# Block turns on VectorE in place of TensorE turns for sixteen row tiles of a sparse attention layer

## The chip, the cores and the metric

The kernel runs on one core of one Trainium2 chip. A core has five engines that run side by side, each through its own list of instructions in order: TensorE (PE in the profile; its weight loads are PEld), VectorE (DVE), ScalarE (ACT), GpSimd (POOL) and SyncE (SP), which here only issues transfers. Transfers are queued by SP, ScalarE or GpSimd and run on 16 DMA engines. Data lies in SBUF, 128 partitions wide; TensorE writes to PSUM, from which VectorE and ScalarE read.

The metric is the device time of one execution in microseconds.

## The reference

The input x has 2708 rows of 1024 numbers, adj is a 2708 by 2708 matrix of zeros and ones in which about 0.15% are ones (some four in a row), and there are three 1024 by 1024 weights with biases.

```python
h = jnp.maximum(_layernorm(x, axis=-1), 0.0)
q = h @ W_q.T + b_q
k = h @ W_k.T + b_k
v = h @ W_v.T + b_v
z = (1.0 / math.sqrt(1024)) * (q @ k.T)
spare_z = z * adj_tensor
spare_z = jnp.where(spare_z == 0.0, -10000.0, spare_z)
attn = jax.nn.softmax(spare_z, axis=1)
x = x + jax.nn.relu(attn @ v)
```

All but a few entries of a row of attn vanish, so a row of the result is a weighted sum of the few rows of h that adj names, times W_v.

## The kernel before, in words

**Stages.** First W_q and W_k are multiplied into one matrix M (lines 433 to 588). Meanwhile rows of x are normalised into h (`stats`, `root`, `apply`, `keep`), and VectorE searches the rows of adj for their ones (`found`, L376; `listed`, L389 to L395). Then h times M gives q, the scores are products of q with gathered rows of h (`scores`, L826), the sums u are weighted sums of gathered rows (`sums`, L879), and u times W_v, plus x, is the output. Rows are worked on in tiles of 128; there are 22 tiles.

**Units.** The products h times M and u times W_v run in units of two tiles, `units`, L1160: ten units q for the pairs (0,1) to (18,19), then ten units o for the pairs (6,5), (4,3), (2,0), (1,7), (13,12), (11,10), (14,9), (15,16), (20,17), (18,19), and tile 8 alone at the end. A unit is a 2 by 2 block product after Strassen and Winograd with seven products in place of eight. Each product is a block of eight matmuls (`add_block`, L948). Its left factors are a11, a12 (of the pair's first tile xa), a22 and a21 (of the second, xb), turned so that the 1024 columns lie on partitions, and the sums s1 = a22 + a21, s3 = a11 - a21, s2 = s1 - a11 and s4 = a12 - s2.

**Turning.** `half_turned` (L397) turns half a tile with four matmuls against the unit matrix (L402) into PSUM. `blocks` (L677) makes the factors for a pair: `upper` has a11 and a12 copied to SBUF by ScalarE (L684), `lower` has a22 copied and forms s1 and s3 on VectorE straight from PSUM (L688), and s2 and s4 on VectorE, or on GpSimd for the pairs (2,3) and (4,5) (L701, L702).

**Order.** `multiply` (L982) writes the order of a unit: the blocks on s2, a12, s4, s3, then the next unit's a11 and s1 (`opened`, L953), then a22. Between them it calls `after(i)`, i from 0 to 6 (L1172), which emits all that runs beside: `upper` for the next pair at i = 0 and `lower` at i = 2 (for the next pair of unit 0 at 3 and 4, of unit 3 at 4 and 5, L1200 to L1206), steps of the search (`steps_at`, L735), and `advance(share)` (L937), which hands out the attention stream on VectorE in portions of 20/7 us (q) or 19/7 us (o) a call. VectorE executes in the order in which this is written (`manual_schedule`), ScalarE and GpSimd too in the early part; TensorE, SP, and the others later, are ordered by a planner. When rows are loaded two units ahead (`load_rows`, L1130), the stream is driven on until their tiles are done (L1214).

**Rows.** The early tiles 0 to 7 keep their h tile in SBUF (`kept`, L217) until `natural_rows` (L716) hands them to units 0 to 3. Later q pairs are gathered from `h_dram`. Of the u tiles, those that are used within two units stay in SBUF (`near`, L933); ten others (6, 5, 4, 3, 2, 0, 1, 20, 18, 19) are stored to `u_dram` by SP (L888) and loaded again by SP (L1142). Row tiles share seven buffers (`row_tile`, L198).

**Search loads.** Rows of adj are loaded by SP into three buffers in turn (`loaded`, L342), so the load for one tile waits until the search three tiles earlier has let go of its buffer.

Of the kernel before, what the change touches and what calls it, by code (L numbers as in the profile page):

```python
# [10 lines left out]
FT = mybir.dt.float32  # L11
# [3 lines left out]
AF = mybir.ActivationFunctionType  # L15
# [18 lines left out]
FAR = 20.0  # L34
WIDE = 8
MOMENTS = (0, 1, 2, 3, 6, 7)
ROOT = 32
# [26 lines left out]
def tile_preln_masked_attention(  # L64
# [35 lines left out]

    h_dram = dram.tile([N, D], FT, name="h_dram")
    q_dram = dram.tile([EARLY * P, D], FT, name="q_dram")
    q_late = dram.tile([(BARE - EARLY) * P, D], FT, name="q_late")
# [97 lines left out]
    def stats(group):  # L201
# [6 lines left out]
        for i, t in enumerate(group):  # L208
            t0, n = tiles[t]
            if 15 <= t < 18:  # L210
                xt = work.tile([P, D], FT, tag="q", name=f"x_{t}", bufs=4)
            elif t >= FULL - 1:
                xt = work.tile([P, D], FT, tag="hT", name=f"x_{t}", bufs=2)
            else:
                xt = row_tile(f"x_{t}")
            if t < EARLY:
                kept[t] = xt  # L217
            nc.sync.dma_start(xt[:n], x[t0:t0 + n, :])
            xs.append(xt)
            if t in MOMENTS:  # L220
                continue
            st = stat.tile([P, NH, 6], FT, tag="st", name="st")
            for s in range(NH):
                nc.vector.bn_stats(st[:n, s, :], xt[:n, s * NB:(s + 1) * NB])
            nc.vector.bn_aggr(mv[:n, i, :], st[:n].rearrange("p s k -> p (s k)"))
# [31 lines left out]
    def apply(first, only=range(4)):  # L257

        group, xs, r = normed[first]
        for i in only:  # L260
            if i < len(group):
                n = tiles[group[i]][1]
                nc.scalar.activation(xs[i][:n], xs[i][:n], AF.Relu, bias=r[:n, 4, i:i + 1], scale=r[:n, 3, i:i + 1])

# [410 lines left out]
    behind = []  # L675

    def blocks(xa, xb, eng=None):  # L677

# [7 lines left out]
        def put(name, a, b, op, eng=None):  # L686
            ops[name] = small(name).rearrange("p (c q) -> p c q", q=P)
            step = (eng or nc.vector).tensor_tensor(ops[name], a, b, op=op)  # L688
            if eng is None:
                behind.append(step)  # L690

        def upper():
            held("a11", half_turned(xa, 0))
            held("a12", half_turned(xa, 1))

        def lower():
            held("a22", half_turned(xb, 1))
            a21 = half_turned(xb, 0)
            put("s1", ops["a22"], a21, ALU.add)
            put("s3", ops["a11"], a21, ALU.subtract)  # L700
            put("s2", ops["s1"], ops["a11"], ALU.subtract, eng)  # L701
# [6 lines left out]
    def banks_for(row):  # L708
# [5 lines left out]
        return return_  # L714

    def natural_rows(n):  # L716
        rows_of[n] = [kept.pop(t) for t in (2 * n, 2 * n + 1)]

    natural_rows(0)
    ops_of = {0: blocks(*rows_of.pop(0))}  # L720
# [154 lines left out]
    def sums(t):  # L875
# [8 lines left out]
        g_of.pop(t)  # L884
        if near(t):
            held[t] = u
# [243 lines left out]
    def load_rows(unit):  # L1130
        kind, *pair = unit
        rows = []
        for t in pair:
# [6 lines left out]
            else:  # L1140
                assert t in done, (t, done)
                nc.sync.dma_start(rows[-1], u_dram[t * P:(t + 1) * P, :])  # L1142
        return rows
# [16 lines left out]
    for n, unit in enumerate(units):  # L1160
        kind, ta, tb = unit
        now[0] = n
        if n == FIRST:
            ordered.close()
            ordered.enter_context(tc.manual_schedule(engines={mybir.EngineType.DVE}))
            nc.sync.dma_start(bp_dram, bp_sb[0:1, :])
        turn = n in (0, FIRST - 1)
# [313 lines left out]
```

## Time and profile before

| what | us |
|---|---|
| median of three runs | 644.58 |
| lowest, highest | 644.18, 644.96 |
| span of the profiled execution | 641.9 |
| TensorE busy | 635.2 |
| VectorE busy | 521.9 |
| GpSimd busy | 377.3 |
| ScalarE busy | 279.6 |

The page of the profiled execution gives its span, from the first to the last instruction, 641.9 us; its time with what lies around the span isn't listed apart from the three runs. The granted TensorE clock was 0.998 of full speed.

In the rows below, a line of the chain of waits has the start in us, the length in us, the engine, what is written, the line of the kernel and the count. A row of a timeline has start and length in us, then engine, line, operation, output and inputs, and in brackets how long the engine sat idle just before and what ended that. A group's row ends with busy us, mean ns of one, and the idle time before. A row of waits has the total us, the count and the longest. A row of stretches has from:to, its length, the busy us of PE, PEld, DVE, ACT and POOL with counts, the clock, the share of the DMA engines and GB/s. A row of transfers ends with KB each and the median us from issue to landing.

### The profile page before, as it was taken

To read this page: it belongs to the slowest core of one execution; us is meant where nothing else is said; L and a number is where in the kernel's file an instruction comes from. 1 tells how busy PE (TensorE), PEld (TensorE's weight loads), DVE (VectorE), ACT (ScalarE), POOL (GpSimd) and SP (SyncE) were. 2 spreads that over 40 slices of the span, in tenths; PEclk is the share of its full clock that TensorE was granted. 3 is DMA by queue.
4 is the path that set the end of the run, shared out by engine and by line. 5 is a ranking of instruction groups with operands and counts; after the bars stand their busy time and mean duration, and the time that the engine had idled before them with its cause. 6 is when DMAs were issued, how large, how long until landed. Compare 5 with 4: busy or idle time off the path is not lost.

```text
span 641.9 us, 6381 instructions
## 1 busy us (share of the span) xinstructions
PE 635.2 (99%) x1731; PEld 326.2 (51%) x1731; DVE 521.9 (81%) x1014; ACT 279.6 (44%) x426; POOL 377.3 (59%) x400
## 2 busy tenths in 40 slices
PE   9999999999999999999999999999999999999996
PEld 5777766444544444444444454454454444444442
DVE  5999788997895755998888959997999989989121
ACT  3539974849775622423223132433342344333300
POOL 2649960875858457755735525665685856872431
PEclk9999999999999999999999999999999999999999
DMA  8999997598798969998977998988898989995542
GB/s 338 407 366 314 345 346 295 189 358 301 264 358 317 363 201 404 355 359 257 322 260 275 419 416 267 327 272 255 240 328 272 283 331 304 281 285 125 146 139 95
DMA packets 61986, 189.02 MB, mean 294 GB/s; under 512 B 10701, under 2 KB 11037, under 8 KB 61048
## 3 DMA queue, kind: packets, MB, share of 16 engines
q0 software_dynamic: 27888, 84.95, 41.6%
q1 hardware_dynamic: 29994, 89.36, 37.7%
q10 hardware_dynamic: 4062, 14.24, 5.9%
q8 instruction: 16, 0.26, 0.2%
q14 instruction: 26, 0.21, 0.1%
HBM read 159.81 MB, written 42.31 MB: 315 GB/s over the span
## 4 chain that ended last, share of the span: by engine, by line
PE 98%; DMA 1%; DVE 0%; POOL 0%; POOLq 0%; issue 0%
PE ps L948 45%; PE psy L948 32%; PE ps_y L463 6%; PE pt L402 6%; PE ps_x L463 4%; PE ps_z L463 4%; DMA wlow<-in_wq_dram 1%; PE ps_h L1153 0%; PE ps_v L581 0%; DVE y_alone L1297 0%; POOL out_dram L1281 0%; POOLq L1303 0%; PE ps_all L664 0%; PE ps_in L662 0%; PE ps_b L728 0%
## 5 line engine op out<-in xcount | busy, mean ns | idle before, releaser
L597 POOL DMA_INDIRECT g<-h_dram,tab x105 | 124.8, 1188 | 70.4 <-ACT u L871 19.1
L948 PE MATMUL ps<-M,a 128*128 128x512 f32 x320 | 144.0, 593 | 0.0
L948 PE MATMUL psy<-wlow,s 128*128 128x512 f32 x320 | 143.9, 592 | 0.0
L826 DVE SCALAR_TENSOR_TENSOR junk<-g,pq 128x1024 uint8<-128x1024 f32 x93 | 114.0, 1226 | 9.8 <-DMA g<-h_dram,tab 7.3
L879 DVE SCALAR_TENSOR_TENSOR u<-g,coef,u 128x1024 f32<-128x1024 f32 x79 | 101.4, 1283 | 5.6 <-ACT u L871 3.7
L948 PEld LDWEIGHTS ps<-M,a 128*128 128x128 f32 x320 | 59.3, 190 | 68.0 <-issue 67.4
L948 PEld LDWEIGHTS psy<-wlow,s 128*128 128x128 f32 x320 | 59.2, 190 | 66.8 <-issue 65.8
L376 DVE FIND_INDEX8 at<-ones,adj 128x8 uint32<-128x685 f32 (+1 forms) x88 | 74.5, 865 | 0.0
L948 PE MATMUL psy<-wlow,a 128*128 128x512 f32 x160 | 71.9, 592 | 0.0
L948 PE MATMUL ps<-M,s 128*128 128x512 f32 x160 | 71.9, 592 | 0.0
L948 PE MATMUL ps<-wlow,s 128*128 128x512 f32 x160 | 71.9, 592 | 0.0
L355 ACT ACTIVATE sized<-adj 128x2708 uint8<-128x2708 f32 (+1 forms) x22 | 54.3, 2468 | 7.7 <-DMA adj<-in_adj_dram 6.4
L285 POOL TENSOR_TENSOR hsum<-hsum,x 128x256 f32<-128x256 f32 (+1 forms) x56 | 38.6, 726 | 26.3 <-DVE wlow L431 22.3
L1047 POOL DMA_INDIRECT y<-in_x_dram,tab x19 | 33.5, 1763 | 30.8 <-ACT taken L1013 11.2
L948 PEld LDWEIGHTS psy<-wlow,a 128*128 128x128 f32 x160 | 30.4, 190 | 38.3 <-issue 37.8
L948 PEld LDWEIGHTS ps<-wlow,s 128*128 128x128 f32 x160 | 30.4, 190 | 38.3 <-issue 37.6
L948 PEld LDWEIGHTS ps<-M,s 128*128 128x128 f32 x160 | 30.3, 190 | 38.1 <-issue 37.4
L778 POOL DMA_INDIRECT out_dram<-y,tab x21 | 28.4, 1353 | 19.3 <-DMA y<-in_x_dram,tab 11.6
L684 ACT COPY a<-pt 128x512 f32<-128x512 f32 x60 | 33.4, 590 | 3.1 <-PE pt L402 3.1
L597 POOL DMA_INDIRECT M<-h_dram,tab x20 | 24.2, 1212 | 13.4 <-ACT u L871 4.7
L688 DVE TENSOR_TENSOR s<-a,pt 128x512 f32<-128x512 f32 x40 | 25.6, 681 | 7.8 <-ACT a L684 7.8
L871 ACT ACTIVATE u<-g,coef 128x1024 f32<-128x1024 f32 x16 | 18.4, 1149 | 27.1 <-DVE coef L870 26.3
(238 smaller groups left out, 847.9 us busy)
## 6 DMA issues: line engine op xcount, KB each, us to landing
adj<-in_adj_dram SPq DMA_DIRECT2D x21, 1354.0 KB, 12.0
x<-in_x_dram SPq DMA_DIRECT2D x21, 512.0 KB, 8.0
h_dram<-x ACTq DMA_DIRECT2D x21, 512.0 KB, 7.2
q_late<-q SPq DMA_DIRECT2D x12, 512.0 KB, 6.9
pq<-q_late SPq DMA_DIRECT2D x12, 512.0 KB, 4.8
u_dram<-u SPq DMA_DIRECT2D x10, 512.0 KB, 6.5
or<-u_dram SPq DMA_DIRECT2D x10, 512.0 KB, 8.2
g<-in_wv_dram SPq DMA_DIRECT2D x16, 256.0 KB, 8.3
```

Source lines behind the costliest of these rows:

```text
L285: small.append(nc.gpsimd.tensor_add(hsum[:n, cols], hsum[:n, cols], xt[:n, cols]))
L355: nc.scalar.activation(sized[:n], a[:n, :, :PW], AF.Abs, accum_out=total[:n, t:t + 1])
L376: nc.vector.max_index(at[:n, k - first_k, g, :], ones[:n, 0:8], a[:n, g, :])
L402: nc.tensor.transpose(pt[:, c, :], xt[:, k * P:(k + 1) * P], ident)
L463: mm = nc.tensor.matmul(bank, a_tile(o + H * a[0], a[1], i), b(o), start=first and o == 0, stop=(o == H - 1), skip_group_check=True)
L597: return nc.gpsimd.indirect_dma_start(out=dst, out_offset=None, in_=src, in_offset=off, bounds_check=N - 1, oob_is_err=False)
L684: nc.scalar.copy(ops[name], bank)
L778: to = nc.gpsimd.indirect_dma_start(out=out, out_offset=bass.IndirectOffsetOnAxis(ap=ptab.bitcast(U32)[:n, t, SLOTS:SLOTS + 1], axis=0), i ...
L826: chained(lambda: nc.vector.scalar_tensor_tensor(junk, g_of[t][s], 1.0, tq[t], op0=ALU.mult, op1=ALU.mult, accum_out=zall[:, t, s:s + 1]))
L879: chained(lambda: nc.vector.scalar_tensor_tensor(u, g_of[t][s], coef[:, at[t][s]:at[t][s] + 1], u, op0=ALU.mult, op1=ALU.add))
L948: mm = nc.tensor.matmul(bank, a[:, c, :], b[:, c, :], start=False, stop=(c == 3), skip_group_check=True)
L1047: return nc.gpsimd.indirect_dma_start(out=y[:n], out_offset=None, in_=x, in_offset=off, compute_op=ALU.add)
```

## The change

Sixteen tiles are turned in another way: the early h tiles 2 to 7 and the ten u tiles that go through DRAM. ScalarE writes a copy of such a tile with its columns in another order, by quarters, and stores it from its own queue: for the h tiles a second `apply` into a row tile and then `hv_dram`, for the u tiles a copy into a row tile and then `u_dram`. SP loads the tile back in four transfers of 128 KB, one for each 32 partitions, each row of 256 numbers from another quarter of the rows (`by_quarters`). VectorE then turns half a tile at a time with one transpose of 32 by 32 blocks (`faces`), straight into the buffers of a11, a12, a22 and, for a21, the buffer of s3.

For pairs with a turned xb, s1 = a22 + a21 and s3 = a11 - a21 then read both inputs from SBUF. s2 and s4 go to GpSimd for every pair with a turned tile. Pairs (2,3), (4,5) and (6,7) are loaded into two buffers of a new pool, so `upper` and `lower` move to steps 3 and 4 in units 0 and 1 and to 2 and 3 in unit 2. The stream's portion is smaller by 0.75/7 us for each turned tile in the next o pair.

```diff
+QUADS = 4
+QP = P // QUADS
+FACED = (6, 5, 4, 3, 2, 0, 1, 20, 18, 19)
@@ apply
+                if 2 <= group[i] < EARLY:
+                    v = row_tile(f"hv_{group[i]}")
+                    nc.scalar.activation(v.rearrange("p (a c r) -> p c a r", a=QUADS, r=QP),
+                                         xs[i].rearrange("p (c a r) -> p c a r", a=QUADS, r=QP),
+                                         AF.Relu, bias=r[:n, 4, i:i + 1], scale=r[:n, 3, i:i + 1])
+                    nc.scalar.dma_start(hv_dram[group[i] * P:(group[i] + 1) * P, :], v)
@@ new functions
+    def by_quarters(dst, rows):
+        faced.append(dst)
+        for a in range(QUADS):
+            cols = slice(a * D // QUADS, (a + 1) * D // QUADS)
+            nc.sync.dma_start(dst[a * QP:(a + 1) * QP, :].rearrange("r (g j) -> r g j", g=QUADS),
+                              rows[:, cols].rearrange("(g r) j -> r g j", r=QP))
+    def faces(dst, xt, lo, hi):
+        return nc.vector.transpose(dst.rearrange("p c (g r) -> p g c r", r=QP),
+                                   xt.rearrange("p (g c r) -> p g c r", g=QUADS, r=QP)[:, :, lo:hi])
@@ blocks
+        def faced_half(name, xt, s):
+            ops[name] = small(name).rearrange("p (c q) -> p c q", q=P)
+            faces(ops[name], xt, s * 4, s * 4 + 4)
         def upper():
-            held("a11", half_turned(xa, 0))
-            held("a12", half_turned(xa, 1))
+            for s, name in enumerate(("a11", "a12")):
+                if is_faced(xa):
+                    faced_half(name, xa, s)
+                else:
+                    held(name, half_turned(xa, s))
         def lower():
+            if is_faced(xb):
+                faced_half("a22", xb, 1)
+                faced_half("s3", xb, 0)
+                put("s1", ops["a22"], ops["s3"], ALU.add)
+                behind.append(nc.vector.tensor_sub(ops["s3"], ops["a11"], ops["s3"]))
+            else:
                 ...
@@ natural_rows
-        rows_of[n] = [kept.pop(t) for t in (2 * n, 2 * n + 1)]
+        rows_of[n] = []
+        for t in (2 * n, 2 * n + 1):
+            rows_of[n].append(quart.tile([P, D], FT, tag="quart", name=f"hq_{t}", bufs=2))
+            by_quarters(rows_of[n][-1], hv_dram[t * P:(t + 1) * P, :])
@@ sums
-        if near(t):
+        if t in FACED:
+            v = row_tile(f"v_{t}")
+            nc.scalar.copy(v.rearrange("p (a c r) -> p c a r", a=QUADS, r=QP),
+                           u.rearrange("p (c a r) -> p c a r", a=QUADS, r=QP))
+            nc.scalar.dma_start(u_dram[t * P:(t + 1) * P, :], v)
+        elif near(t):
             held[t] = u
@@ load_rows
+                if t in FACED:
+                    by_quarters(rows[-1], u_dram[t * P:(t + 1) * P, :])
+                else:
+                    nc.sync.dma_start(rows[-1], u_dram[t * P:(t + 1) * P, :])
@@ units
+        if nxt is not None and nxt[0] == "o":
+            share -= 0.75 / 7 * len(set(nxt[1:]) & set(FACED))
-                if i == (3 if n == 0 else 4 if turn else 0):
-                    ops_of[n + 1] = blocks(*rows_of[n + 1], nc.gpsimd if n + 1 < FIRST - 1 else None)
+                if i == {0: 3, 1: 3, 2: 2, FIRST - 1: 4}.get(n, 0):
+                    ops_of[n + 1] = blocks(*rows_of[n + 1], nc.gpsimd if n + 1 < FIRST - 1 or any(
+                        is_faced(xt) for xt in rows_of[n + 1]) else None)
-                if i == (4 if n == 0 else 5 if turn else 2):
+                if i == {0: 4, 1: 4, 2: 3, FIRST - 1: 5}.get(n, 2):
                     ops_of[n + 1][2]()
```

More of the change, by code (lines that the diff above doesn't have):

```diff
@@ L101, in tile_preln_masked_attention @@
     h_dram = dram.tile([N, D], FT, name="h_dram")
+    hv_dram = dram.tile([EARLY * P, D], FT, name="hv_dram")
     q_dram = dram.tile([EARLY * P, D], FT, name="q_dram")
@@ L714, in banks_for @@
         return return_
+    quart = search.enter_context(tc.tile_pool(name="quart", bufs=1, side="left"))
     def natural_rows(n):
-        rows_of[n] = [kept.pop(t) for t in (2 * n, 2 * n + 1)]
-    natural_rows(0)
+        rows_of[n] = []
+        for t in (2 * n, 2 * n + 1):
+            rows_of[n].append(quart.tile([P, D], FT, tag="quart", name=f"hq_{t}", bufs=2))
+            by_quarters(rows_of[n][-1], hv_dram[t * P:(t + 1) * P, :])
+    rows_of[0] = [kept.pop(t) for t in range(2)]
     ops_of = {0: blocks(*rows_of.pop(0))}
```

15 lines of the change are left out of this document (8 added, 7 removed).

## The prediction

> **What bounds the kernel now.** I read the page's first and fourth parts, then the chain of waits in order of time, the groups of instructions, and VectorE's timeline and waits for the two stretches that the change touches.
>
> ```profile
> span 641.9 us, 6381 instructions
> ...
> PE 635.2 (99%) x1731; PEld 326.2 (51%) x1731; DVE 521.9 (81%) x1014; ACT 279.6 (44%) x426; POOL 377.3 (59%) x400
> ...
> PE 98%; DMA 1%; DVE 0%; POOL 0%; POOLq 0%; issue 0%
> ```
>
> TensorE never waits: the chain is one matmul after another. So an instruction taken from it is worth its length, as long as what it waits for keeps up. VectorE has 19% idle over the whole span, but not where it matters. The chain shows the turns that go, and two places to remember:
>
> ```profile
> 176.56 3.43 PE psy L948 x8
> 180.00 6.87 PE ps L948 x16
> ...
> 501.57 0.87 PE pt L402 x8
> ...
> 517.06 6.87 PE ps L948 x16
> ...
> 604.71 0.88 PE pt L402 x8
> ```
>
> A tile's eight turns take 0.87 us of TensorE. A block of eight products takes 3.43. At 180.00 the first block on a11 of tiles 6 and 7 starts. At 517.06 a11 of tiles 14 and 9 starts, and 3.43 later, at 520.49, the block on their s1.
>
> **Term 1, TensorE.** Tiles 2 to 7 of the early rows and the ten u tiles lose their eight turns each: 16 x 0.87 = 13.9 us. Nothing is added to TensorE. The profiled execution has a span of 641.9; the median of the runs, 644.58, is 2.7 above it, and I leave that difference as it is. With nothing else the time would be 630.7.
>
> **Prices of what is added.** Block turns are not in this trace. The nearest rows, and those of the parts that move:
>
> ```profile
> L826 DVE SCALAR_TENSOR_TENSOR junk<-g,pq 128x1024 uint8<-128x1024 f32 x93 | 114.0, 1226 | 9.8 <-DMA g<-h_dram,tab 7.3 <-DMA pq<-q_dram,tab 0.7
> ...
> L684 ACT COPY a<-pt 128x512 f32<-128x512 f32 x60 | 33.4, 590 | 3.1 <-PE pt L402 3.1
> ...
> L263 ACT ACTIVATE x<-x,r 128x1024 f32<-128x1024 f32 x21 | 24.8, 1234 | 7.1 <-POOL r L253 7.1
> ...
> L224 DVE BATCH_NORM_STATS2 st<-x 128x6 f32<-128x512 f32 x30 | 18.7, 665 | 0.0
> ...
> L688 POOL TENSOR_TENSOR s<-a,s 128x512 f32<-128x512 f32 x2 | 2.5, 1271 | 0.2
> ```
>
> A half-tile turn reads 512 numbers per partition. VectorE's one-input row of that size is 0.665 us; the timeline below has two operations of that size in 1.27, so 0.635 from start to start, which I take. The upper bound is 1.22, the row that goes over 1024 numbers, as if each number were passed twice. There are 32 such turns: 12 early, 20 late.
>
> s2 and s4 of pair (6,7) and of the six late pairs with a turned tile go from VectorE (0.635) to POOL (1.27). That looks like relief, but two rows speak against it:
>
> ```profile
> 132.78 1.26 POOL L688 TENSOR_TENSOR s<-s,a 128x512 f32<-128x512 f32 x1
> 134.12 1.27 POOL L688 TENSOR_TENSOR s<-a,s 128x512 f32<-128x512 f32 x1
> ```
> ```profile
> 132.93 1.26 DVE L389 TENSOR_TENSOR cand<-first,at 128x128 f32<-128x128 f32 x1
> 134.22 1.31 DVE L390 SCALAR_TENSOR_TENSOR cand<-at,cand 128x128 f32<-128x128 uint32 x1
> ...
> 174.24 0.09 DVE L376 MATCH_VALUE_LOAD at<-ones,adj 128x8 f32 x1 [1.89 <-DMA adj<-in_adj_dram]
> ...
> 177.74 0.29 DVE L389 TENSOR_TENSOR cand<-first,at 128x128 f32<-128x128 f32 x1
> 178.07 0.29 DVE L390 SCALAR_TENSOR_TENSOR cand<-at,cand 128x128 f32<-128x128 uint32 x1
> ...
> 180.85 1.27 DVE L688 TENSOR_TENSOR s<-a,pt 128x512 f32<-128x512 f32 x2
> ```
>
> The same two VectorE operations take 0.29 each alone and 1.26 and 1.31 while POOL forms s2 and s4: 2.0 us lost. Late in the kernel nearly all of VectorE's work has two inputs in SBUF (L826, L879), so I charge 2.0 a pair; bounds 0 (POOL runs beside block turns) and 2.54 (both operations whole). Moving the pair saves VectorE 1.27 and costs it 2.0.
>
> The Trainium skill ("SBUF — State Buffer", SBUF: two separate sides) says that a VectorE instruction with two SBUF inputs and a GpSimd instruction that reads SBUF need the same port pair, and that whichever starts second blocks fully. The rows at 132.93 agree. By the rule's full block the four late pairs of term B would lose 4 x 0.54 = 2.2 more, and the sum would be 643.9.
>
> **Term A, the early stretch.** The search (L376) and the products share VectorE's written order. Its waits from 106.98 to 180.9:
>
> ```profile
> DVE q L1029 <- PE psy L948: 1.9, 1, 1.9
> DVE at L376 <- DMA adj<-in_adj_dram: 1.9, 1, 1.9
> DVE s L688 <- ACT a L684: 1.3, 2, 0.7
> ```
> ```profile
> 165.69 0.54 SPq L347 DMA_DIRECT2D adj<-in_adj_dram  x1
> ```
>
> Before a11 of (6,7) is there, VectorE has nine more turns to do: eight of pairs (2,3) and (4,5), one of its own, 9 x 0.635 = 5.7. The waits for ScalarE's copies and for TensorE (1.3 + 1.9) take up 3.2. The wait for adj stays: its load is issued at 165.69, when VectorE has done with the buffer, so it moves along. The turns stand behind the search of that tile in the written order (unit 2, step 2), so a11 comes at 180.85 + 5.7 - 3.2 = 183.3. Before, a11 came from TensorE and ScalarE and asked VectorE for nothing. TensorE, six tiles lighter (5.2), wants it at 174.8: a wait of 8.5 us. The a22 block of that unit (3.43) needs none of it and can run first if the planner puts it there; TensorE's order is not written by hand. That leaves 5.1, and I add 0.9 for POOL's adds of hsum beside s1 and s3, which now have two SBUF inputs. **A = 6**, bounds 3 (the adj wait goes as well) and 12 (no swap, adj 2 us later).
>
> **Term B, the attention stretch.** VectorE's waits from 346.9 to 436.4, then the stretch after it and the two points that frame it:
>
> ```profile
> DVE junk L826 <- DMA g<-h_dram,tab: 5.3, 3, 2.1
> DVE s L688 <- ACT a L684: 3.4, 2, 2.2
> DVE u L1063 <- PE ps L948: 1.7, 1, 1.7
> DVE m L861 <- ACT w L860: 0.5, 1, 0.5
> DVE q L1029 <- PE psy L948: 0.2, 1, 0.2
> ```
> ```profile
> 436.31 0.69 DVE L1063 TENSOR_TENSOR u<-ps,u 128x512 f32<-128x512 f32 x1 [1.68 <-PE ps L948]
> ...
> 519.39 1.28 DVE L688 TENSOR_TENSOR s<-a,pt 128x512 f32<-128x512 f32 x2
> ```
> ```profile
> 436.31:520.49 84.18, 84.18 (x233) 39.85 (x232) 78.59 (x120) 29.68 (x51) 59.77 (x45) 1.00 0.90 285
> 520.49:604.71 84.22, 84.22 (x235) 39.87 (x234) 71.91 (x127) 29.95 (x54) 47.27 (x35) 1.00 0.80 238
> ```
>
> At 436.31 VectorE had caught up with TensorE. From there it is busy 78.6 of 84.2 us, and s1 of (14,9) is ready at 520.03, 0.5 before TensorE takes it. That is all the room there is. Up to 436 VectorE gets 14 turns (8.9), is rid of eight s operations (-5.1), loses four pairs to POOL (+8.0), and has 4.9 of the stream put off by the smaller share (0.75 a tile: 3 x 1.5, and 0.4 by then in unit 12): +6.9. Against that stand the waits for ScalarE and TensorE (3.4 + 1.7 + 0.2) and half of those for gathers (2.6): -7.9, so 1.0 earlier. The 4.9 put off come back before s1 of (14,9), because loading those rows drives the stream on until both are done; 1.0 of the remaining waits goes. s1 is then ready at 520.03 - 1.0 + 4.9 - 1.0 = 522.9. TensorE, seven tiles lighter (6.1), wants it at 514.4: a wait of 8.5. With the a22 block put ahead, 5.1. A shifts both sides alike. **B = 5**, bounds 0 (all waits of both stretches go, POOL costs nothing) and 12.
>
> **At nothing.** The last three turned tiles (20, 18, 19) give VectorE 3.8 - 2.5 + 4.0 = 5.3 us in a stretch with 12.3 idle (last row above), and TensorE leaves 2.6 less; were that idle gone, 8 us would show at 604.71. ScalarE loses 25 copies (14.8) and gains six applies and ten copies of the same size, 16 x 1.23 = 19.7, at 44% busy; what queues behind a copy that waits for its tile's last sum are the evictions for TensorE. Transfers:
>
> ```profile
> h_dram<-x ACTq DMA_DIRECT2D x21, 512.0 KB, 7.2
> ...
> u_dram<-u SPq DMA_DIRECT2D x10, 512.0 KB, 6.5
> or<-u_dram SPq DMA_DIRECT2D x10, 512.0 KB, 8.2
> ```
> ```profile
> 154.12 2.37 ACT L263 ACTIVATE x<-x,r 128x1024 f32<-128x1024 f32 x2
> ```
>
> Sixteen stores sit on ScalarE's queue (ten leave SP's). SP issues 64 quarter loads for 10 whole ones, ahead of adj loads in its order. A store and a load take 7.2 + 8.2 = 15.4 (a u tile's 6.5 + 8.2), and rows 6 and 7 have the 27 us from their apply at about 155 to VectorE's turn at 182. They cost nothing unless SP stands at an adj wait. Then VectorE stands at the turn, with the search and the evictions c12 and c22 behind it; that adds to A, inside its bound. On POOL the gathers queue behind s2, which waits for s1, and VectorE's scores wait for the gathers. I put that at nothing, as most of those gathers need a buffer that VectorE frees after s1; if not, waits like the 5.3 us above grow, inside B's bound.
>
> **Sum.** 644.6 - 13.9 + 6 + 5 = 641.7.
>
> **Rivals.**
> *Full gain.* VectorE fits everything into its waits: 630.7 to 635. For it: 120 us idle in the span. Against: 0.5 us of room at 520.
> *No swap (slower).* The place is a11 of (6,7) and s1 of (14,9): the planner leaves the a22 block behind the late one and TensorE stands 9.4 and 8.5 us: 644.6 - 13.9 + 9.4 + 8.5 = 648.6. It decides from 13.9 us of waiting in all. For it: in every unit of the chain a22 comes last.
> *A wash.* One swap of the two: 641.7 + 3.4 = 645.1.
> *Turns at 1.22.* Each costs 0.585 more: nine in A, 14 in B, 13.5 us: 655. The Trainium skill ("VectorE: DVE Perf Modes", The three transpose paths) gives 311 ns for 128x128 in bf16; four of these make 1.24 for a half tile, as an estimate, which is this rival. No run here shows a block turn yet; the rows of 512 inputs speak for the lower price.
>
> **How the numbers follow.** Forecast 0.42, full gain 0.08, wash 0.12, no swap 0.32, dear turns 0.06. A change under 0.2% (1.3 us) can't be told from none. Faster 0.50, same 0.12, slower 0.38. The forecast's own range is 637 to 643.3; with the bounds of A and B, and leaving out the dearest tenth and the full gain, 634 to 651.
>
> **What would show it.** The page should have 128 fewer turns on TensorE and 32 turns on VectorE at 0.6 to 0.7. The chain should leave TensorE near 175 to 183 for a VectorE turn, and once more near 515. L826 and L879 should stretch beside POOL's L688. If TensorE stays at 98% of the chain, A and B are wrong; if the chain runs through SP or a quarter load, the round trip was not hidden.

## The result and the profile after

The changed kernel takes 654.84 us (median of 5 runs, 651.88 to 657.11) beside 644.18 (643.80 to 644.96) for the kernel before: a ratio of 1.0156, 95% interval 1.0142 to 1.0170. So it is slower, by 1.6%. The forecast was 641.7, with 634 to 651. The profiled execution took 652.5 with a span of 650.8, so 8.9 us longer in its span.

The page of the changed kernel, its first and fourth parts:

```profile
span 650.8 us, 6276 instructions
...
PE 626.2 (96%) x1603; PEld 313.9 (48%) x1603; DVE 543.3 (83%) x1032; ACT 285.3 (44%) x417; POOL 400.6 (62%) x414
...
PE 62%; DVE 19%; DMA 10%; issue 5%; POOL 1%; ACT 1%; SPq 0%; POOLq 0%; DVEq 0%; ACTq 0%
```

TensorE has 128 matmuls fewer (1731 to 1603), as the change wants, and the chain of waits now leaves it for VectorE and for transfers. What TensorE waited for, all of it over 0.5 us (its waits: what waited, for what, us in total, times, longest):

```profile
PE ps L999 <- DVE a L699: 9.5, 2, 9.0
PE ps L999 <- DMA M<-in_wv_dram: 3.1, 1, 3.1
PE psy L999 <- ACT u L1043: 1.9, 1, 1.9
PE ps_y L508 <- POOL hsum L116: 1.2, 1, 1.2
PE psy L999 <- DMA wlow<-tv_dram: 0.9, 1, 0.9
PE ps_in L672 <- DVE sort L660: 0.8, 1, 0.8
PE ps L999 <- ACT ps L754: 0.8, 1, 0.8
PE ps L999 <- DVE s L716: 0.6, 1, 0.6
PE ps_x L473 <- DMA wlow<-in_wq_dram: 0.6, 1, 0.6
```

Without the two at the start (1.2 and 0.6, in the kernel before 1.2 and 0.3), TensorE stands still 17.6 us. Behind its start the kernel before does not stand still at all. The longest wait, in the chain in order of time (start, length, what):

```profile
169.18 10.12 DVE at L386 x12
...
179.35 8.29 DMA adj<-in_adj_dram
...
187.69 0.72 DVE a L699
...
188.55 8.65 PE ps L999 x16
```

The reader is to see VectorE in twelve lookups of the search (L386) and, last, the turn of (6,7) that the product at 188.55 needs. What lies between is better read from VectorE's timeline, as the load of 8.29 is one for a later search:

```profile
181.02 0.09 DVE L386 MATCH_VALUE_LOAD at<-ones,adj 128x8 f32 x1 [1.73 <-DMA adj<-in_adj_dram]
...
187.69 1.90 DVE L699 STREAM_TRANSPOSE a<-hq 128x512 f32<-128x512 f32 x3
```

VectorE waits 1.73 us for the adj of one more tile, searches it from 181.02 to 187.69 without a pause, and only then turns. The second place, in the chain again:

```profile
371.76 0.34 SPq L1073
...
372.19 16.59 DMA M<-in_wv_dram
...
388.82 8.83 PE ps L999 x16
```

Here SP asks for a block of weights behind a store of q, and the block takes 16.6 us to land.

Both times something else was lost. The windows around the first hole (stretch, length, TensorE busy, granted clock, DMA share, GB/s):

```profile
180.00:184.00 4.00, 0.00 (x0) 1.00 1.03 399
184.00:188.00 4.00, 0.00 (x0) 0.61 1.02 347
188.00:192.00 4.00, 3.45 (x5) 0.54 0.98 334
```

At the first hole (a stretch in which TensorE stands still) the granted clock falls to half at 184.8, before the products come, and stays there for the first of them. At the second it falls only at 389.6, when they have been running for 0.8 us. The eight at 188.55 take 5.22 us and the eight at 388.82 take 5.40, where eight take 3.60 at full clock. That loses 1.6 and 1.8, 3.4 together.

So the sum of the profiled execution is: 13.9 saved, 17.6 of standing still, 3.4 of half clock, +7.1. The span grew by 8.9. Of the 1.8 between, some 1.4 is an estimate from the rows: a row of eight products is 3.60 us long, but the next row starts 3.43 behind its start, so each of the eight holes cost about 0.17 more than its own length. The rest I can't assign.

### The profile page after: what moved, and what is told of

The parts are those of the page before. It is cut to its first block, busy times and chain, and to the rows that moved or that the text cites. A ratio compares the mean times of both kernels' runs of the same rounds, so it can differ in the third digit from the quotient of the medians.

```text
span 650.8 us, 6276 instructions
## 1 busy us (share of the span) xinstructions
PE 626.2 (96%) x1603; PEld 313.9 (48%) x1603; DVE 543.3 (83%) x1032; ACT 285.3 (44%) x417; POOL 400.6 (62%) x414
## 4 chain that ended last, share of the span: by engine, by line
PE 62%; DVE 19%; DMA 10%; issue 5%; POOL 1%; ACT 1%; SPq 0%; POOLq 0%; DVEq 0%; ACTq 0%
PE ps L999 26%; PE psy L999 19%; DVE u L925 7%; PE ps_y L473 6%; PE ps_x L473 4%; PE ps_z L473 4%; DVE junk L872 4%; DVE at L386 4%; DMA adj<-in_adj_dram 3%; DMA M<-in_wv_dram 3%; PE pt L412 2%; DMA x<-in_x_dram 2%; DMA hq<-hv_dram 1%; DVE s L716 1%; DVE a L699 1%
## 5 line engine op out<-in xcount | busy, mean ns | idle before, releaser
L999 PE MATMUL ps<-M,a 128*128 128x512 f32 x320 | 147.5, 604 | 13.4 <-DVE a L699 9.5
L607 POOL DMA_INDIRECT g<-h_dram,tab x105 | 127.0, 1210 | 52.9 <-issue 17.8
L872 DVE SCALAR_TENSOR_TENSOR junk<-g,pq 128x1024 uint8<-128x1024 f32 x93 | 115.9, 1246 | 2.8 <-DMA pq<-q_dram,tab 1.0
L925 DVE SCALAR_TENSOR_TENSOR u<-g,coef,u 128x1024 f32<-128x1024 f32 x79 | 106.1, 1343 | 5.2 <-ACT u L917 3.1
L999 PEld LDWEIGHTS ps<-M,a 128*128 128x128 f32 x320 | 60.9, 194 | 86.7 <-issue 70.6
L386 DVE FIND_INDEX8 at<-ones,adj 128x8 uint32<-128x685 f32 (+1 forms) x88 | 74.5, 865 | 0.0
L1098 POOL DMA_INDIRECT y<-in_x_dram,tab x19 | 30.7, 1618 | 16.1 <-issue 4.7
L623 POOL DMA_INDIRECT tab_dram<-tab,pos_i x22 | 22.3, 1011 | 10.6 <-issue 5.8
L273 ACT ACTIVATE x<-x,r 128x1024 f32<-128x1024 f32 (+1 forms) x22 | 26.2, 1232 | 5.7 <-POOL r L257 3.2
L473 PE MATMUL ps_y<-wlow 128*128 128x512 f32 x64 | 27.6, 592 | 0.0
```

What stands on the lines that cost most here:

```text
L386: nc.vector.max_index(at[:n, k - first_k, g, :], ones[:n, 0:8], a[:n, g, :])
L473: mm = nc.tensor.matmul(bank, a_tile(o + H * a[0], a[1], i), b(o), start=first and o == 0, stop=(o == H - 1), skip_group_check=True)
L607: return nc.gpsimd.indirect_dma_start(out=dst, out_offset=None, in_=src, in_offset=off, bounds_check=N - 1, oob_is_err=False)
L623: put = nc.gpsimd.indirect_dma_start(out=tab_dram[lo >= EARLY][:, :], out_offset=bass.IndirectOffsetOnAxis(ap=pos_i[:n, t:t + 1], axis=0), ...
L872: chained(lambda: nc.vector.scalar_tensor_tensor(junk, g_of[t][s], 1.0, tq[t], op0=ALU.mult, op1=ALU.mult, accum_out=zall[:, t, s:s + 1]))
L925: chained(lambda: nc.vector.scalar_tensor_tensor(u, g_of[t][s], coef[:, at[t][s]:at[t][s] + 1], u, op0=ALU.mult, op1=ALU.add))
```

## The experiments

The kernel before took 644 us on three of the chips used and 648 to 649 on two others, so each ratio below is to the kernel before on the same chip. "TensorE's holes" are its waits in the profiled execution. No trace of the kernel before on the two slower chips is kept. But all kernels that ran there with the early part as before (e5, e6, e7, e9, e10, e12) have holes of 1.9 to 5.0 us together between 180 and 207, and e1 and e18, on faster chips, have none there.

**e1: the u tiles alone.** The early six are kept and turned by TensorE as before.

```diff
-            if t < 2:
+            if t < EARLY:                  # tiles kept in SBUF
...
-                if 2 <= group[i] < EARLY:  # hv and its store: left out
...
+        rows_of[n] = [kept.pop(t) for t in (2 * n, 2 * n + 1)]
```

> Only the ten u tiles are turned by VectorE; the early six are kept and turned by TensorE as before. Theory (the parts add): at ps_h TensorE was 10.3 us late in the changed kernel, all from the early part, and 8.9 at the end, so the late part is worth about -1.4: 643 here; the hole of 3.9 us ahead of the products by M near 380 stands, 10 us earlier. Rival (attention is late again): without the early delay s1 of (14,9) is due 10 us earlier and VectorE's wait of 5 to 8.5 near 515 comes: 648 to 652, with a hole of that size ahead of that pair's products.

Measured: 643.51 us, ratio 0.9996 (0.9974 to 1.0019). TensorE's waits beyond the start:

```profile
PE ps L987 <- DMA M<-in_wv_dram: 3.0, 1, 3.0
PE pt L405 <- DVE u L913: 2.1, 1, 2.1
```

The parts add, as the theory had it: ten tiles save 8.7, the two holes cost 5.1 and the half clock behind each together 3.3. The rival has part of the truth too: VectorE is late near 507, by 2.1 and not by 5 to 8.5.

**e2: the early tiles alone.**

```diff
-FACED = (6, 5, 4, 3, 2, 0, 1, 20, 18, 19)
+FACED = ()
```

> Only the six early h tiles are turned by VectorE; the u tiles go as before. Theory (the parts add): the hole of 9.0 us at 188.55, the shorter ones near 106 and 150 to 155 and the half clock after it stand; 10.3 us late at ps_h and nothing regained: about 654.5. Rival (the late part costs in the changed kernel, by its hole of 3.9 and the slow products behind it, and the delay is partly taken up by later waits): 648 to 651.

Measured: 655.45 us, ratio 1.0191 (1.0167 to 1.0214). The early part by itself costs as much as the whole change: 11.5 us, which with the 0.5 that e1 gains makes 11.0, and the change as a whole has 10.7. TensorE stands still 12.3 us, with 2.7 lost to half clock, for 5.2 saved. The holes are the early ones of the changed kernel (106, 150 to 155 and 188), the longest again the turn of (6,7):

```profile
PE ps L999 <- DVE a L699: 8.7, 2, 8.2
```

**e3: the search behind the turns of (6,7).** The changed kernel with search step 17 at another place.

```diff
-                ... (1, 6): "f16 p15", (2, 1): "f17",
+                ... (1, 6): "f16 p15",
-                ... (2, 5): "f18 f19 p19", ...
+                ... (2, 5): "f17 f18 f19 p19", ...
```

> The changed kernel, with the search step 17 (four lookups and its list, 6.6 us on VectorE) moved in VectorE's written order from ahead of the turns of (6,7) to behind the last addition of unit 2. Theory (the hole at 188.55 is the written order): a11 of (6,7) is turned at about 179.4 instead of 187.69, the hole of 9.0 falls below 1.5 and the granted clock stays at full there: 8 to 10 us faster than the changed kernel, 643 to 646. Rival (the delay is only moved): the search, 7 us later, holds unit 3's additions or the counts, or the attention that the delay had covered is late again: 650 or more.

Measured: 650.81 us, ratio 1.0107 (1.0090 to 1.0124), 3 us less than the changed kernel by ratio where 8 to 10 were expected. The hole at 188.55 is gone: the turns come at 178.95 and the products by (6,7) start at 181.26 with no wait. So the written order did make it. But a new hole stands at 195, and the eight products behind it take 6.56 us, nearly all at half clock:

```profile
PE psy L999 <- ACT psy L1012: 3.4, 1, 3.4
```

```profile
189.31 2.46 ACT L365 ACTIVATE sized<-adj 128x2708 uint8<-128x2708 f32 x1 [0.41 <-ACT x L273]
...
191.90 2.46 ACT L365 ACTIVATE sized<-adj 128x2708 uint8<-128x2708 f32 x1
...
194.36 0.58 ACT L1012 COPY psy<-ps 128x512 f32<-128x512 f32 x1
```

ScalarE's timeline shows why: in its written order two passes that count rows of adj stand ahead of the copy that TensorE now wants 7 us earlier.

**e13: the counts behind as well.**

```diff
-                (2, 4): "p18", (2, 5): "f17 f18 f19 p19", (2, 6): "f20 p20",
+                (2, 5): "f17 f18 f19", (2, 6): "p18 p19 f20 p20",
```

> As e3 (the changed kernel, search step 17 behind), and ScalarE's passes that count rows 18 and 19 moved behind its copies of psy and p of unit 3. Theory (with the search moved, the hole of 3.4 to 5.9 us at 195 is ScalarE's order): it closes, with the half clock behind it: 3.4 to 6 us less than e3, which is 3.1 us below the changed kernel by ratio (1.0107 against 1.0156): ratio to the kernel before 1.002 to 1.006. Rival (the lateness goes on to the next wait, such as the normalisation that POOL computes): 1.008 to 1.012.

Measured: 652.51 us, ratio 1.0129 (1.0111 to 1.0147), no better than e3. The rival is right in kind, though the next wait is not the one it named:

```profile
PE pt L412 <- DMA qr<-h_dram,tab: 4.4, 1, 4.4
```

The hole at 195 closes (2.0 us at 181.8, for VectorE's turn, are left), and TensorE stands at 207 for the gathered rows of unit 4. The kernel before had no room there to begin with: POOL asks for the first of these rows at 192.70, they land at 200.28, and TensorE turns them at 200.43. Three orders meet here (VectorE's search, ScalarE's counts, the gathers by POOL), and TensorE's gain of 5.2 runs into each of them in turn.

**e11: of the early tiles only the last pair.** Tiles 6 and 7 on VectorE with the search moved as in e3, all else as in the kernel before.

```diff
-            if t < 2:
+            if t < 6:
-                if 2 <= group[i] < EARLY:
+                if 6 <= group[i] < EARLY:
...
+        rows_of[n] = [kept.pop(t) for t in (2 * n, 2 * n + 1)] if n < 3 else []
```

> Of the early six only tiles 6 and 7 are turned by VectorE, with search step 17 behind them as in e3; everything else as in the kernel before. Theory (the holes at 106 and 149 to 156 and VectorE's waits for adj there come of the quarter loads and turns of tiles 2 to 5): none of these holes; what is left is below 4 us near 190, and the time is within 2 us of the kernel before, ratio 0.998 to 1.003. Rival (one pair is enough to make the early part late): holes of 4 us or more and a ratio above 1.005.

Measured: 652.90 beside 648.74, ratio 1.0054 (1.0036 to 1.0073). The holes at 106 and 149 to 156 are gone, as the theory had it, so they come of tiles 2 to 5. By its middle value the rival is right on the sum: one pair is enough, with 5.9 us behind ScalarE's copies at 196. Not all of the 5.9 is the pair's: on this chip the kernels with the early part as before stand 1.9 us at that copy (e9, e10, e12); the ratio leaves out what both kernels share.

What makes VectorE late between 105 and 190 is seen in its waits, first of the changed kernel, then of e11:

```profile
DVE at L386 <- DMA adj<-in_adj_dram: 6.6, 3, 4.6
```
```profile
DVE at L386 <- DMA adj<-in_adj_dram: 1.3, 1, 1.3
```

and in SP's queue in the changed kernel (start, us from first to last issue, count):

```profile
133.23 9.24 SPq L694 DMA_DIRECT2D hq<-hv_dram  x8
142.58 10.19 SPq L357 DMA_DIRECT2D adj<-in_adj_dram  x4
```

Eight quarter loads hold SP for 9.2 us, and the loads of adj that the search needs stand behind them. The longest of the three waits, 4.6 us, ends at 147.94, for one of these. In the kernel before the same wait for adj comes to 1.9 us between 105 and 190, and with only one pair turned to 1.3. Whether the order on SP alone makes the difference was not tried by itself.

**e15: the swap.** The changed kernel with the a22 block of unit 2 ahead of unit 3's first products on TensorE.

```diff
-        between(n)
-        add_block(Y, ops["a22"], T[:, 3])
-        results[3](Y)
+        if n == 2:
+            last = add_block(Y, ops["a22"], T[:, 3])
+            results[3](Y)
+            with tc.issue_after(last.ins):
+                between(n)
+        else: ...
```

> The changed kernel, with the eight products by a22 of unit 2 put ahead of the first products of unit 3 in TensorE's order: the swap that the prediction left to the planner. Theory (the hole is VectorE's lateness, which a swap shortens by 3.4): the hole of 9.0 at 188.55 becomes 5.6, and the time is 3 to 4 us less than that of the changed kernel beside it. Rival (TensorE gains nothing, as the next unit waits for the same chain): the same time as the changed kernel within 1.5 us.

Measured: 660.35 us, ratio 1.0257 (1.0240 to 1.0275), 6.1 us more than the changed kernel beside it (e16). The hole grows to 13.1, and its row with VectorE's rows ahead of it say why:

```profile
192.94 6.42 PE L999 MATMUL psy<-wlow,a 128*128 128x512 f32 x8 [13.09 <-DVE q L1086]
```
```profile
187.65 1.90 DVE L699 STREAM_TRANSPOSE a<-hq 128x512 f32<-128x512 f32 x3
...
192.20 0.68 DVE L1086 TENSOR_TENSOR q<-psy,p 128x512 f32<-128x512 f32 x1
```

The a22 block adds into the bank psy, which VectorE's c22 must have read first, and c22 stands behind the late turns in VectorE's order. With that order the swap can't help, and the planner's order was the better one. Both theories fall. A c22 ahead of the turns was not tried.

> The changed kernel again, beside the others on the same chip. By its first runs: ratio 1.0156, a hole of 9.0 near 188, holes of 0.9 and 3.1 near 382 and 389.

Measured: 654.26 us, ratio 1.0168 (1.0133 to 1.0203), with a hole of 9.9 at 189.0 and holes of 0.7 and 3.1 near 382 and 389.

**e8 and e17: the hole filled.** The changed kernel with products of no use ahead of the first product of unit 3, 19 in e8 and 9 in e17.

```diff
+        if n == 2:
+            fill_ps = psum.tile([P, NB], FT, tag="tp", name="fill_ps")
+            for i in range(9):
+                with tc.issue_after(products[-1].ins):
+                    filled = nc.tensor.matmul(fill_ps, ident, bp_sb[:, :NB], start=True, stop=True)
...
```

> The changed kernel, with 19 products of no use (identity by a row tile, 8.2 us) on TensorE in the hole ahead of the first product of (6,7). Theory (the granted clock halves because TensorE stood still): the clock stays at full from 180 to 200, the first eight products behind the hole take 3.6 us instead of 5.2, and the time falls by 1.5 to 3.4: 651 to 653. Rival (the slow products have another cause, such as operands that are still being written or traffic): they take 5.2 as before, and the time is 654 to 656.

Measured: ratio 1.0130 (1.0086 to 1.0175) on another chip, clock at full from 180 to 200. The filling lasted 16.5 us, so its time says little.

> As e8, with 9 products of no use instead of 19 (in e8 each took two passes, 0.87 us, and the 38 passes lasted 16.5 us, longer than the hole). 9 fill 7.8 of the 9.0 us. Theory (TensorE's standing still halves the clock): full clock from 180 to 200, 3.6 us for the eight products behind the hole instead of 5.2, and 1.6 to 3.4 us less than the changed kernel beside it. Rival: 5.2 us for them and no gain.

Measured: 655.44 us, ratio 1.0184 (1.0167 to 1.0201), against 1.0168 (1.0133 to 1.0203) in e16: no gain. But the clock is what the theory says, in e17's windows and TensorE's rows:

```profile
188.00:192.00 4.00, 4.00 (x11) 1.00 0.95 355
```
```profile
181.08 7.89 PE L1058 MATMUL fill_ps<-bp_sb,ident 128*128 128x512 f32 x18
188.81 3.60 PE L999 MATMUL ps<-M,a 128*128 128x512 f32 x8
```

The same products start at the same time (188.81, in e16 189.05) and take 3.60 us instead of 5.22. So it is standing still that halves the clock here. In the profiled execution of e17 the 1.6 us were lost again, as the clock was halved from 156.3 on, behind the short holes at 154 and 155, where it had stayed full in e16.

**e4: the weights ahead of the store.** The changed kernel; the first store of the last q pair is asked for with the second.

```diff
-            if ta >= EARLY:
+            if EARLY <= ta < BARE - 2:
                 store(qa, ta)
...
-            if ta < EARLY:
+            if ta < EARLY or ta == BARE - 2:
                 store(qa, ta)
```

> The changed kernel, with the stores of q of the last pair asked for after its last result, so that on SP the two loads of M stand ahead of the first of them. Theory (the holes of 0.86 and 3.07 near 382 and 389 are these loads waiting on SP behind a store that waits for VectorE): the loads are issued 6 to 7 us earlier, both holes close, and the eight products behind them take 3.6 us instead of 5.4: about 5.5 us faster than the changed kernel, 649. Rival (the transfers are late by themselves, beside the quarter loads, or the next loads take their place): within 1.5 us of the changed kernel, 653 to 656.

Measured: 659.24 us, ratio 1.0238 (1.0221 to 1.0255). In the profiled execution (652.1 us) the waits for M fall from 3.1 to 0.7, but the next weights are late in their place:

```profile
PE psy L999 <- DMA wlow<-tv_dram: 2.6, 1, 2.6
...
PE ps L999 <- DMA M<-in_wv_dram: 0.7, 2, 0.4
```

So the queue moves the hole and the transfers hold it; this is the rival's mechanism, though not its 653 to 656. All of e4's timed runs but the profiled one lie near 659. Their granted clock was lower, 0.984 to 0.988 against 0.992, which over a span of 657 us makes up to about 4 of the 7 us (an estimate); the rest stays open. The windows of the kernel before and of the changed one show the transfers full in both (share 1.02 and 1.05) and moving less in the second:

```profile
370.00:380.00 10.00, 10.00 (x37) 5.36 (x36) 4.67 (x9) 2.26 (x5) 2.80 (x2) 1.00 1.02 415
```
```profile
370.00:380.00 10.00, 10.00 (x25) 4.46 (x24) 9.86 (x11) 1.61 (x2) 8.02 (x8) 1.00 1.05 303
```

415 GB/s before, 303 with the quarter loads under way, in rows of 1 KB. They bring tiles 4 and 3. The kernel before loads the same two tiles whole, asked for earlier, at 340.48 and 347.94.

**e5, e6, e7, e10: fewer u tiles, and s2 and s4 back on VectorE.** All on the kernel of e1.

```diff
 e5:  +FACED = (6, 5, 2, 0, 1, 20, 18, 19)
 e6:  +FACED = (2, 0, 1, 20, 18, 19)
 e7:  -... nc.gpsimd if n + 1 < FIRST - 1 or any(is_faced(xt) for xt in rows_of[n + 1]) else None
      +... nc.gpsimd if n + 1 < FIRST - 1 else None
 e10: both e5 and e7
```

> As e1 (u tiles alone), but tiles 4 and 3, whose quarter loads stand on SP ahead of the loads of M, are turned by TensorE again. Theory (the hole of 3.02 us at 378 is the quarter loads of this pair, on SP and in transfers that are full there): it closes, and the half clock behind it with it, 4.7 us; TensorE pays 1.7 for the two tiles, and as it comes to 507 earlier than VectorE gains there, the hole of 2.07 stays or grows by 2: 640 to 643, with no wait for M. Rival (M is late by itself): the hole near 378 stands and the time is 643.5 plus 1.7: 645.

Measured: 647.71 beside 648.21, ratio 0.9989 (0.9975 to 1.0003). No wait for M is left, while e7, on the same chip with the quarter loads of 4 and 3, has one of 1.9: these loads made it. The wait for VectorE's sum near 510 grows from 2.1 to 3.0, with 3.0 of half clock behind it. Kernels without these loads ask for 4 and 3 whole at the same place in SP's order, so two of them on one chip, e12 with quarter loads and e10 without, show what the transfers lose (e1 and e5 have 315 and 421 GB/s there):

```profile
360.00:370.00 10.00, 10.00 (x25) 1.00 1.05 331
```
```profile
360.00:370.00 10.00, 10.00 (x24) 1.00 1.02 422
```

> As e1, but tiles 6, 5, 4 and 3 are all turned by TensorE again; six u tiles are left to VectorE. TensorE pays 3.5 us. Theory: the hole at 378 and its half clock are gone (4.7), VectorE has 5.4 us of turns less ahead of 507 and the hole there is below 1: 638.5 to 641.5. Rival (VectorE's lateness at 507 is not of the turns but of what TensorE reaches earlier): a hole of 4 us or more near 505 and 643 or more.

Measured: 648.13 beside 648.21, ratio 0.9993 (0.9973 to 1.0013). Neither theory's number: instead of one hole near 507 there are four from 502 to 606, 4.1 us together.

> As e1, but s2 and s4 of the turned u pairs are computed by VectorE, as of the other u pairs, instead of POOL. Theory (an operation of two operands on POOL holds VectorE for its length, about 1.0 to 1.2 us each): VectorE pays 1.4 us a pair and gets 2.0 to 2.4 back, the hole of 2.07 at 507 shrinks: 641 to 643.5, and no score or sum of VectorE is stretched beside POOL. Rival (the stretched operations cost VectorE less than the two it takes over): VectorE is 5 us later at 507, and the time is 646 to 649.

Measured: 644.46 beside 648.21, ratio 0.9946 (0.9915 to 0.9977). The hole at 508 is 0.3, but e12 below, on the other of the slower chips, shows the same with s2 and s4 on POOL, so it can't be put down to the edit. What the edit does is seen in VectorE's groups by form, first e1, then e7 (busy us, mean ns):

```profile
L860 DVE SCALAR_TENSOR_TENSOR junk<-g,pq 128x1024 uint8<-128x1024 f32 x93 | 115.9, 1246 | 3.7 <-DMA g<-h_dram,tab 1.1 <-DMA pq<-q_dram,tab 0.8
L913 DVE SCALAR_TENSOR_TENSOR u<-g,coef,u 128x1024 f32<-128x1024 f32 x79 | 106.1, 1343 | 5.2 <-ACT u L905 3.1 <-ACT u L899 0.2
...
L709 DVE TENSOR_TENSOR s<-a,s 128x512 f32<-128x512 f32 x16 | 11.1, 692 | 0.9
```
```profile
L860 DVE SCALAR_TENSOR_TENSOR junk<-g,pq 128x1024 uint8<-128x1024 f32 x93 | 113.8, 1224 | 2.8 <-DMA pq<-q_dram,tab 0.9
L913 DVE SCALAR_TENSOR_TENSOR u<-g,coef,u 128x1024 f32<-128x1024 f32 x79 | 101.4, 1283 | 5.2 <-ACT u L905 3.1 <-ACT u L899 0.2
...
L709 DVE TENSOR_TENSOR s<-a,s 128x512 f32<-128x512 f32 x22 | 15.2, 692 | 1.3
```

Scores and sums are 8.2 us longer beside POOL (2.1 and 4.7 in these rows, 1.4 in the scores that read M), 1.4 a pair. (e12, on another chip than e1, has 116.0 and 106.1 in these rows.) The twelve operations cost VectorE 12 x 0.68 = 8.2. The two are equal, so it makes no difference to VectorE's busy time where s2 and s4 are computed.

> Eight u tiles (without 4 and 3) on VectorE, s2 and s4 on VectorE too. Theory (the two causes among the u tiles are separate): no wait for M near 380, TensorE then reaches 507 to 527 some 3 us earlier and waits there 2 to 4 us for VectorE: 3 us less than the kernel before on the same chip, ratio 0.995 to 0.996. Rival (nothing else is late): 6 to 7 us less, ratio 0.99.

Measured: 646.71 beside 648.74, ratio 0.9959 (0.9941 to 0.9977), 2.0 us less where the theory had 3: the theory, with 3.0 us of waiting at 511 and 3.0 lost to half clock behind it.

> The kernel of e1 again, beside the others on the same chip. By e1: ratio 0.9996, holes at 378 (M) and 507 (u).

Measured: 646.32 beside 648.74, ratio 0.9956 (0.9940 to 0.9973), where the same kernel had 0.9996 as e1. On this chip TensorE already stood 3.1 us between 192 and 205, in work that e1 and the kernel before share, and reached the holes at 380 and 508 later, so they are shorter (2.4 and 0.3; a wait of 1.2 for one of VectorE's sums s stands at 524).

**e9, e18, e14: only the last three u tiles.** 20, 18 and 19 on VectorE, s2 and s4 too.

```diff
-FACED = (6, 5, 4, 3, 2, 0, 1, 20, 18, 19)
+FACED = (20, 18, 19)
```

> Only the last three u tiles of the change (20, 18, 19) are turned by VectorE; s2 and s4 on VectorE, the early six as before. Theory (what the change costs lies in the early part, in the loads near 380 and in VectorE's lateness up to 530, none of which these three touch): 2.6 us less than the kernel before on the same chip, ratio 0.996, and no new hole. Rival (their round trip or their turns hold the last units): a hole behind 570 and a ratio of 1 or more.

Measured: 645.75 beside 648.74, ratio 0.9943 (0.9927 to 0.9960), no hole behind 200 (3.2 us between 180 and 194, in work that the kernel before shares).

> The kernel of e9 (tiles 20, 18 and 19 alone on VectorE) in five rounds, on whatever chip comes. Theory: 2.6 us less than the kernel before, ratio 0.996, on a chip where that takes 644 us as on one where it takes 648. Rival: the gain of e9 belongs to the chip, and the ratio is 0.999 or more.

Measured: 641.31 (640.90 to 641.77) beside 644.18, ratio 0.9958 (0.9944 to 0.9972). This beats both kernels. Its page:

```profile
span 639.2 us, 6353 instructions
...
PE 99%; POOL 0%; DVE 0%; POOLq 0%; issue 0%
```

TensorE has 24 matmuls fewer and never waits; 2.7 of span and 2.9 of time are gone for 2.6 expected.

> e9 with ScalarE's counts of rows 18 and 19 behind its copies of psy and p of unit 3. Theory by e13 (lateness there goes on to the gather of unit 4's rows): no gain over e9 beside it, a ratio between 0.995 and 1.0, with a hole near 205. Rival: the hole of 1.87 near 194 closes and nothing follows: ratio 0.992.

```diff
-                (2, 4): "p18", (2, 5): "f18 f19 p19", (2, 6): "f20 p20",
+                (2, 5): "f18 f19", (2, 6): "p18 p19 f20 p20",
```

Measured: 642.16, ratio 0.9967 (0.9955 to 0.9980), with a new hole of 1.2 at 202 for gathered rows: the theory by e13.

## Why the prediction was wrong

**Term 1 was right.** 128 matmuls went, 13.9 us. e18 shows the term alone: three tiles, 2.6 forecast, 2.7 measured.

**The price of a turn was right.** The rows of the changed kernel, by form; three turns take 1.90 us (the row at 187.69), 0.63 each, where 0.635 was forecast from two operations in 1.27:

```profile
L699 DVE STREAM_TRANSPOSE a<-or 128x512 f32<-128x512 f32 x16 | 10.6, 692 | 0.0
```

The rival with 1.22 falls. So does its estimate from the Trainium skill ("VectorE: DVE Perf Modes", The three transpose paths): its 311 ns for 128x128 gave 1.24 for a half tile, and the trace has half of that.

**The price of POOL's s2 and s4 was too high.** 2.0 a pair was charged and 1.4 measured (e1 against e7), which is what moving them saves. The rule of the Trainium skill ("SBUF — State Buffer", SBUF: two separate sides), by which whichever starts second blocks fully, would have given up to 2.54; over the six pairs the runs show little more than half of that on VectorE. POOL pays as well: its eight s4 take 1.84 us on average in e1, where the two of the kernel before take 1.27.

**Term A is where the prediction fell.** It had VectorE's place right: the turns of (6,7) stand behind a search and TensorE waits for them, 9.0 us where the prediction had 8.5 without a swap. That these are so close is luck. The first turn was done at 188.4 instead of 183.3, and TensorE, held up before, wanted it at 179.5 instead of 174.8. The 0.9 for POOL's adds did not show: s1 and s3 take 0.69 us each at 190.32. Three steps were wrong.
- The a22 block "needs none of it and can run first". It needs the bank that c22 reads, and c22 stands behind the same turns in VectorE's written order (e15: 13.1 us instead of 9.0). In this order that 3.4 was not to be had.
- "They cost nothing unless SP stands at an adj wait", of the transfers. It came the other way round: the quarter loads were in time, and the loads of adj came late behind them on SP. VectorE's waits for adj between 105 and 190 went from 1.9 to 6.6, about what the turn came too late. The holes at 154 and 155 (1.4 us) stand behind the same search.
- A was taken as the whole of the early delay. The holes at 106 and 149 (2.6 us) were in no term: ScalarE's copies come there when they came in the kernel before (105.79 and 149.18, before 105.66 and 149.21), and TensorE, lighter by its turns, is there earlier. e3, e11 and e13 show more of this: behind VectorE's order stand ScalarE's counts and the gathers of unit 4, which had 0.15 us of room. With the search moved TensorE still kept none of its 5.2 (the early holes of e3 are 7.3 us), and with the counts moved too no more (e13).

In all the early part stands still 13.0 us (9.0 and 4.0), against an A of 6 with an upper bound of 12.

**Term B had about the size, but not the place, so its size is luck.** Forecast 5 (8.5 without a swap). Between 340 and 535 the changed kernel stands still 4.5 us and loses 1.8 to half clock, 6.3 in all; but only 0.6 of it is s1 of (14,9), and the rest is the weights at 382 and 389. "They cost nothing" failed there too: the transfers were full at that place already (share 1.02). Where the weights are on time (e5, e10), VectorE's lateness comes out at 510. Seven tiles ahead of 530 save 6.1, and the variants that turn them on VectorE lose 5.1 (e7), 5.6 (e12) and 8.4 (e1) there, half clock included; 1.2, 1.2 and 3.8 of this stands behind VectorE and nearly all the rest behind the weights. Whichever is late first takes what TensorE gains. VectorE's part is the room of 0.5 us at 520 that the prediction read from the trace.

**The half clock was in no term**: 3.4 us in the profiled execution.

In spans the forecast was 639.0 (641.7 less the 2.7 that it left as they were) and 650.8 came. Of the 11.8 between them A is 7.0, the half clock 3.4 and the 1.8 beside the holes the rest; B takes 0.5 off.

**The last three at nothing was right** (e9 and e18, with s2 and s4 on VectorE). In the changed kernel, where POOL computes them, TensorE has no hole behind 531 either.

The rival "no swap" (648.6, chance 0.32) names what happened at a11 of (6,7), but at its other place, s1 of (14,9), TensorE waited 0.6 us and not 8.5. Of the rivals "Turns at 1.22" (655) lies nearest in number, and its mechanism is the one that fell most clearly.

## What to carry to other kernels

Where one engine never waits, work taken from it is worth its length only up to the next engine's slack at that place, not its slack over the span: read the slack from the rows that are needed at the same moment, one unit at a time. Here it was 0.15 us at 200 and 0.5 at 520, and 12 in the stretch behind 520; moving the last three tiles alone gave what they cost TensorE. Before a reordering is counted as a rescue, ask for its output bank: who must have read it, and behind what does that reader stand. And a new load is not free because its data come in time: it stands ahead of other loads on its queue, and in small pieces it slowed transfers that were full (331 GB/s instead of 422).

## What the hardware showed that I had not expected

The granted clock goes to half behind holes far shorter than the longest, but not always. The same hole of 1.87 us, at the same place, in e9 and in e6:

```profile
193.90 5.40 PE L987 MATMUL psy<-wlow,s 128*128 128x512 f32 x8 [1.87 <-ACT psy L1000]
```
```profile
192.60 3.70 PE L987 MATMUL psy<-wlow,s 128*128 128x512 f32 x8 [1.87 <-ACT psy L1000]
```

Of six kernels with this hole two lost 1.7 us behind it (e7, e9) and four did not (e5, e6, e10, e12). The half clock lasts 3.4 us or a multiple of it (3.4, 6.8, 10.2, 13.7 in these traces, but for the one at each end).

The clock records of the traces go further. In one trace all half-clock stretches start whole multiples of 3.413 us apart: in e15 at 150.67, 184.80, 393.02 and 522.72, that is 10, 61 and 38 of them. Cut each of the twenty traces along its own grid of 3.413 us. Where TensorE was idle for 1.95 us or more of a piece at full clock, half clock followed all 25 times; for less than 1.80, never (86 pieces with 0.3 us or more); in between, both (four of ten). So it counts how much of a hole falls into one piece. The 1.87 us of e6, e7, e9 and e12 lie in one piece each, at the limit; those of e5 and e10 are cut in two (0.8 and 1.1, 0.6 and 1.2), and so is e4's hole of 2.58, which cost no half clock either (0.9 and 1.7).

The Trainium skill ("TensorE: Matmul & The Clock Gate", Part 1: The HAM clock gate) describes a free-running window of 3.4 us; the lengths agree. Its rule that gaps over some 3.4 us are what bites (HAM oscillation) is too mild by these rows. The phase of the grid differs from trace to trace, which may be why kernels with holes scatter (651.9 to 657.1 for the changed one, 640.9 to 649.2 for e1, while e18, without a hole, lies within 0.9 us). The granted clocks of the runs bear that out only in part: the changed kernel's slowest run had 0.984 and its others 0.988 to 0.991, but e1's slowest had 0.996 and its fastest 0.995.
